# A four-part convolution kernel: attention weights carried to the lanes by DMA through DRAM, and the steps of the attention part ordered anew

## The chip, the cores and the metric

The kernel runs on one core of a Trainium2 chip. A core has five engines, each with its own stream of instructions taken in order: TensorE (PE, matrix products; its weight loads, PEld, overlap them), VectorE (DVE), ScalarE (ACT, functions from tables), GpSimd (POOL) and SyncE (SP, which here only issues transfers). Sixteen DMA engines move data between DRAM, which holds inputs, outputs and scratch tensors, and SBUF, the 128-lane working memory. Products are written to PSUM, eight banks of 512 floats a lane. Engines wait for each other on semaphores. The metric is the time of one execution in microseconds (us); smaller is better.

## What is computed

The input x is 8 images of 16 channels and 128 x 128 pixels, float32. Four layers follow, each of the form x = x + layer(group_norm(x)). The change lies in the first. For each pixel it takes the 3 x 3 window (wrapped at the border) as three tokens (the columns j of the window) of 48 numbers each (three rows, 16 channels), runs a small transformer block over the three tokens, and sums them:

```python
x = _fold_to_kernels(in_x)                     # [B*H*W, 3 tokens, 48]
h = _ln(x)
q, k, v = jnp.split(h @ w_attn.T, 3, axis=-1)  # then 4 heads of 12
att = jnp.einsum('nhtd,nhsd->nhts', q, k) * (1.0 / np.sqrt(HEAD_DIM))
att = jax.nn.softmax(att, axis=-1)
y = jnp.einsum('nhts,nhsd->nhtd', att, v)
x = x + y @ w_attn_proj.T
h = _ln(x)
x = x + jax.nn.gelu(h @ w_fc.T, approximate=False) @ w_fc_proj.T
x = _ln(x)
x = jnp.sum(x, axis=1).reshape(B, H, W, N_EMBD)
out = jnp.einsum('bhwc,oc->bohw', x, conv_w) + conv_b[None, :, None, None]
```

The second layer gates the pixels by two 1 x 1 convolutions, the third is a convolution of rational functions, the fourth one of splines. Their code does the same work in both kernels.

## The kernel before

Attention works in 32 steps of four image rows (`Step`, one chunk of 512 pixels per image). Lanes hold two images of 64 lanes each (48 used); four image pairs `k` make two halves `d`, each a tile of 128 lanes and 2 x 512 columns. A token `u` (0 to 2) of all four pairs is three half-tiles; so a step has six units, numbered `i = 3 d + u`.

The stages of a step are methods. `load` brings the input rows into `xin` (24 transfers of 32 KB). `center` (L441) multiplies by weights that also apply the group norm and subtract the mean; ACT copies the result and squares it. `first` adds the squares into the variances. `scaled` spreads the reciprocal deviation to all lanes and multiplies (DVE); `qkv` makes q, k and v in three products, copied out by ACT, with the wrapped border columns of k and v by POOL, and the differences `dv` of neighbouring columns of v. `multiply` (L483) forms q times the five shifted k, on POOL in the even middle. `scores` adds them over a head's lanes by PE into PSUM banks 1 and 0. `softmax` (L510) copies score rows together so that each of 96 rows has its three partners, subtracts the maximum, takes exponentials, adds (POOL), takes the reciprocal and multiplies (DVE). Only two of three weights are needed, since the three sum to one: y is the middle v plus weighted differences.

`attend` (L532) spreads the weights of one image pair `k` and one side `j` to the 128 lanes: three matmuls with a selection matrix `spread` into three banks; DVE multiplies by `dv` out of PSUM (L543), and POOL subtracts (L551) or adds (L553) to form y. There are eight such calls a step. `project` (L556) multiplies y by the projection weights, and DVE adds the centred input; `square` and `vary` feed the second variance. `normed`, `hidden` (two products of 128 outputs and one of 64, each with a gelu on ACT) and `back` are a unit of the second half; `unit` is a generator over them. The same squares and variances serve the last norm; `narrow` and `finish` apply the output weights and the last norm, `store` adds the input and writes the rows to the scratch tensor `x1d`.

All variances of a step (four kinds, of three steps at once) lie in one bank, and `Variances.finish` turns them into `rstd` by logarithm, exponential and two DVE operations. `place` says at which lane and row a variance lies: four groups of 32 lanes.

`two()` hands out pairs of banks in a ring of three pairs (two pairs while `attend` holds banks 1 to 3). A pair that is handed out again must first be emptied by ACT or DVE.

The main loop (L688) writes out the order of PE by hand: `in_turn` chains PE's instructions, and DVE's and POOL's heavy ones, in the order in which they are recorded. The other instructions are placed by a scheduling layer, which also sets each engine's final order. In one pass of the loop `new` is in attention, `old` in its last units and `then` in its q, k, v and scores, `ahead` in its centring. Eight slots `between` put the work of `old` (units 4 and 5) beside the eight `attend` calls, and projections, squares, variances and q, k, v of the next step behind them; after `rstd` come units 0 and 1 of `new` with the scores of `then`, its softmax beside unit 2, and unit 3.

ACT holds one table of functions at a time: `lut` (L143) orders the gelus and the exponentials and logarithms in phases, and a change of phase is a table load.

At the start, weights are loaded on ACT's queue (L297 to L319); the weights of the second part (`w1s`, 40 small blocks) and the biases are put into the list `loads`, which goes out on SP's queue in step 0 (L734).

Of the kernel before, what the change touches and what calls it, by code (L numbers as in the profile page):

```python
# [22 lines left out]
E = 48  # L23
# [13 lines left out]
def _constants():  # L37
# [19 lines left out]
    score = np.zeros((128, 56))  # L57
    score[token, 24 + 4 * g + h] = 1.0
    parts["score"] = score
    spread = np.zeros((128, 4, 128))  # L60
    bcast = np.zeros((128, 5, 128))
    last = np.zeros((128, 2, 2, 32))
    for t in range(4):
        bcast[32 * t + 16 + g, 4, token] = 1.0
        for n in range(4):
            bcast[32 * t + 4 * (n // 2) + 2 * (n % 2) + g, n, token] = 1.0
            spread[32 * t + 8 * n + 4 * g + h, n, token] = 1.0
        for u in range(2):
            for k in range(2):
                last[32 * t + 8 + 4 * u + 2 * k + g, u, k, 16 * g + c] = 1.0  # L70
    parts["spread"] = spread.reshape(128, 512)
    parts["bcast"] = bcast.reshape(128, 640)
# [33 lines left out]
def kernel(  # L106
# [29 lines left out]
    from_ = _WHERE["pair"][1]  # L136
    const = cpool.tile([128, _CONST.shape[1] - from_], F32, name="const")
    nc.scalar.dma_start(const, const_in[:, from_:])

    def k_(name):  # L140
        n, lo, hi = _WHERE[name]
        return const[:n, lo - from_ : hi - from_]
# [83 lines left out]
    w1s, b1s = [], []  # L226
    for n in range(5):
        t = cpool.tile([BC, BC], F32, name=f"w1_{n}")
        nc.gpsimd.memset(t, 0.0)
        for b in range(B):  # L230
            r = slice(b * C, (b + 1) * C)
            loads.append((t[r, r], w1[n].rearrange("i o -> o i") if n < 2 else w1[n]))
        w1s.append(t)
        b1s.append(rep(b1[n], B, f"b1_{n}"))
# [7 lines left out]
    with ExitStack() as l0:  # L242
# [19 lines left out]
        def k0(name):  # L262
# [4 lines left out]
        spread, bcast = (  # L267
            k0(name).rearrange("p (n m) -> p n m", m=128) for name in ("spread", "bcast")
        )
        last_sel = k0("last").rearrange("p (u k m) -> p u k m", u=2, k=2)  # L270
# [26 lines left out]
        for i in range(3):  # L297
            for g in range(2):
                r = slice(64 * g + i * 16, 64 * g + i * 16 + 16)
                nc.scalar.dma_start(  # L300
                    wqkv[r, :, :E], w0_qkv[i].rearrange("c (n o) -> c n o", n=3)
                )
                nc.scalar.dma_start(wfc[r], w0_fc[i])
                nc.scalar.dma_start(wcv[r, g * 16 : (g + 1) * 16], w0_conv[i])
# [11 lines left out]
        for g in range(2):  # L316
            nc.scalar.dma_start(wpc[64 * g : 64 * g + E, :E], w0_proj)
# [39 lines left out]
        def work(name):  # L357
            return tmp.tile([128, 2, 512], F32, tag="work", name=name, bufs=11)

        def large(name):  # L360
            return tmp.tile([128, 3, 512], F32, tag="large", name=name, bufs=5)
# [22 lines left out]
        def place(k, u):  # L384
            return 32 * (2 * (k % 2) + u % 2), 4 * (u // 2) + 2 * (k // 2)

        class Variances:
# [3 lines left out]
            def __init__(self, first, others):  # L391
                self.due = [first + n * others for n in (4, 2, 4, 2)]
                self.begun = [False] * 4
# [13 lines left out]
            def finish(self):  # L407
                w, pv = work("r0"), banks[:, 0]
                r0, sq = w[:, 0], w[:, 1]
                lut(r0, pv, AF.Ln, bias=eps_t, scale=-2.0)  # L410
# [3 lines left out]
                r = act.tile([128, 512], F32, name="rstd", bufs=2)  # L414
# [3 lines left out]
        class Step:  # L418


            def __init__(self, h0):
# [3 lines left out]
                self.dv = {}  # L425
# [16 lines left out]
            def center(self, d):  # L442
                p = two()
                blocks(p, lambda k: wcen[:, 2 * d + k], xin[:, 2 * d : 2 * d + 2])
                self.xc[d] = act.tile([128, 2, 512], F32, name="xc", bufs=5)
# [4 lines left out]
            def first(self, var):  # L450
                for d in range(2):
                    for k in range(2):
                        var.add(32 * (2 * d + k), 16, self.sq1[d][:, k])

            def scaled(self, d):
                p = two()
                for k in range(2):
                    t = 32 * (2 * d + k)
                    pe(p[:, k], bcast[t : t + 32, 4], self.r1[t : t + 32], start=True, stop=True)
# [3 lines left out]
            def qkv(self, d):  # L463
                q = self.q[d] = work("q")
                self.k[d] = act.tile([128, 8, W + 4], F32, name="kp", bufs=2)
                self.v[d] = act.tile([128, 8, W + 4], F32, name="vp", bufs=2)
                for n, t in enumerate((q, self.k[d], self.v[d])):
# [10 lines left out]
                    else:  # L478
                        copy(t, p)
                self.dv[d] = act.tile([128, 8, W + 4], F32, name="dv", bufs=2)  # L480
# [3 lines left out]
            def multiply(self, d, engine):  # L484

                for k in range(2):
                    parts = []
                    for at, n in ((0, 3), (3, 2)):
                        t = large("pd")
                        ins = (nc.vector if engine == "dve" else nc.gpsimd).tensor_mul(  # L490
                            t[:, :n].rearrange("p n (a b) -> p n a b", a=4),
# [7 lines left out]
            def scores(self, k, which):  # L499

                for i in which:
                    pe(
                        banks[32 * i : 32 * i + 32, 1] if i < 4 else banks[64:96, 0],
                        score[:, 24 - 8 * k : 56 - 8 * k],
# [5 lines left out]
            def softmax(self):  # L510

                a = self.att = act.tile([96, 3, 512], F32, name="att")
                for u in range(3):
                    copy(a[32 * u : 32 * u + 32, 1], banks[32 * u + 32 : 32 * u + 64, 1])
                copy(a[0:64, 2], banks[64:128, 1])
                copy(a[64:96, 2], banks[64:96, 0])
                w = work("mx")
                mx, sm = w[:96, 0], w[:96, 1]
                nc.vector.tensor_max(mx, banks[0:96, 1], a[:, 1])
                nc.vector.tensor_max(mx, mx, a[:, 2])  # L520
                nc.vector.tensor_sub(a[:, 0], banks[0:96, 1], mx)
                for j in (1, 2):
# [1026 lines left out]
```

## Time and profile before

| | |
|---|---|
| median of 3 runs | 10,415.76 us (10,415.72 to 10,424.08) |
| the profiled execution | 10,417.28 us |
| its span, first to last instruction | 10,415.5 us |
| PE busy | 8,808.0 us (85%) |
| DVE, ACT, POOL busy | 8,490.1, 8,595.5, 5,545.7 us |
| mean granted PE clock | 0.979 of full speed |
| first and last `rstd` (attention) | 59.6 and 3,184.9 us |
| first gate product of the second part | 3,213.4 us |
| moved by DMA | 215.74 MB, on average 21 GB/s |

The span is that of one execution; engines overlap in it, so busy times do not add up to it. The page cuts the span into 40 slices and gives each engine's busy share in tenths. Attention fills the first twelve slices, the rational convolution most of the rest. A row of a group of instructions gives the line, engine, operation, output and inputs with shapes, count, total busy us, mean ns of one, and the idle time of the engine before them with what ended it. Almost all matmuls of attention are recorded at one line (L375, the helper `pe`), so they are told apart by the names of their operands.

In the middle of attention, DVE, ACT, POOL and PE are busy 49.1, 52.2, 61.1 and 87.8 us a step (window 1000 to 1096 us). SP issues the 24 input loads in 16.1 us of queue time, and one load and one store of 256 KB.

### The profile page before, as it was taken

What the parts mean: (1) busy time and instruction counts of PE and PEld (TensorE: products, weight loads), DVE (VectorE), ACT (ScalarE), POOL (GpSimd) and SP (SyncE); (2) the same over time, 40 slices, a digit from 0 to 9 for tenths busy, and PEclk for the clock granted to TensorE, in tenths of its full rate; (3) what the DMA queues carried; (4) which work ended last, traced back from release to release, by engine and by line L of the source; (5) the groups of instructions that cost most, each with busy time, mean ns of one, the idle gap of its engine ahead of it and who ended that gap; (6) DMA issues with size and microseconds to landing.
All of it is one profiled execution on the core that took longest, in us unless ns stands there. A gap on an engine that the chain in (4) does not pass through costs nothing.

```text
span 10415.5 us, 192029 instructions
## 1 busy us (share of the span) xinstructions
PE 8808.0 (85%) x81400; PEld 2482.8 (24%) x81400; DVE 8490.1 (82%) x6774; ACT 8595.5 (83%) x7107; POOL 5545.7 (53%) x2608
## 2 busy tenths in 40 slices
PE   6999999999996888888888888888888888888799
PEld 1222222222222222222222222222222222222222
DVE  4545554554555999999999999999999999999977
ACT  3555555555555999999999999999999999999988
POOL 4666666666652555555555555555555555555421
PEclk8999999999998999999999999999999999999999
DMA  1000000000002000000000000000000000000022
GB/s 53 13 15 15 14 14 15 15 13 15 15 7 77 14 21 16 18 21 14 21 14 21 14 20 21 14 21 14 21 14 21 17 18 20 14 13 9 14 62 62
DMA packets 203668, 215.74 MB, mean 21 GB/s; under 512 B 50616, under 2 KB 159416, under 8 KB 200760
## 3 DMA queue, kind: packets, MB, share of 16 engines
q1 hardware_dynamic: 197544, 198.27, 7.0%
q8 instruction: 640, 10.49, 0.4%
q10 hardware_dynamic: 5264, 5.17, 0.2%
q14 instruction: 220, 1.80, 0.1%
HBM read 117.80 MB, written 60.04 MB: 17 GB/s over the span
## 4 chain that ended last, share of the span: by engine, by line
DVE 43%; PE 25%; issue 21%; ACT 8%; DMA 2%; SPq 1%; POOL 0%; DVEq 0%; ACTq 0%; POOLq 0%
PE banks L375 18%; DVE u L1078 15%; DVE pn L1078 10%; DVE u L1082 9%; DVE t L1068 2%; PE pn L1019 2%; PE pd L1019 2%; PE acc L1398 2%; DVE y L543 2%; DVE x L565 1%; ACT hid L157 1%; ACT sq L571 1%; ACT u L157 1%; DMA f<-yd 1%; DVE x L662 1%
## 5 line engine op out<-in xcount | busy, mean ns | idle before, releaser
L1091 POOL TENSOR_TENSOR v<-t,u 128x1280 f32<-128x1280 f32 x1152 | 3449.8, 2995 | 3080.8 <-DVE t L1068 3044.7
L1068 DVE SCALAR_TENSOR_TENSOR t<-t,u 128x2048 f32<-128x2048 f32 x1152 | 2632.7, 2285 | 32.3 <-ACT u L157 31.2
L1019 PE MATMUL pd<-f,wb 32*64 32x512 f32 x18432 | 2510.2, 608 | 92.8 <-ACT t L1057 40.5
L1057 ACT ACTIVATE t<-pd 128x1024 f32<-128x1024 f32 x2304 | 2364.9, 1026 | 133.2 <-PE pd L1019 75.0
L1019 PE MATMUL pn<-f,wa 32*64 32x512 f32 x18432 | 1299.4, 615 | 1112.1 <-DVE u L1082 1111.9
L157 ACT ACTIVATE u<-u 128x2048 f32<-128x2048 f32 x1152 | 2208.9, 1917 | 0.0
L157 ACT ACTIVATE u<-t 128x2048 f32<-128x2048 f32 x1152 | 2204.0, 1913 | 0.0
L1078 DVE TENSOR_TENSOR u<-pn,u 128x1280 f32<-128x1280 f32 x1152 | 1718.8, 1492 | 122.2 <-DVE pn L1078 2.8
L157 ACT ACTIVATE hid<-banks 128x1024 f32<-128x1024 f32 x576 | 569.9, 1023 | 1049.6 <-PE banks L375 1048.3
L1110 PE MATMUL acc<-u,const 128*32 128x512 f32 (+2 forms) x13824 | 1112.1, 454 | 0.0
L1078 DVE TENSOR_TENSOR pn<-pn,u 128x768 f32<-128x768 f32 x1152 | 1103.3, 958 | 0.0
L1082 DVE SCALAR_TENSOR_TENSOR u<-t,pn 128x768 f32<-128x768 f32 x1152 | 1087.6, 944 | 0.0
L1019 PEld LDWEIGHTS pd<-f,wb 32*64 32x64 f32 x18432 | 615.1, 130 | 1249.6 <-ACT t L1057 891.8
L1019 PEld LDWEIGHTS pn<-f,wa 32*64 32x64 f32 x18432 | 275.7, 130 | 2117.2 <-DVE u L1082 2109.7
L1110 PE MATMUL acc<-v,const 128*32 128x512 f32 (+1 forms) x9216 | 763.2, 449 | 1.5 <-POOL v L1091 1.5
L490 POOL TENSOR_TENSOR pd<-q,kp 128x1536 f32<-128x1536 f32 x248 | 674.6, 2732 | 11.2 <-PE banks L375 9.1
L571 ACT ACTIVATE sq<-x 128x1024 f32<-128x1024 f32 x384 | 395.3, 1053 | 272.6 <-DVE x L565 172.8
L375 PE MATMUL banks<-h,wfc 64*128 64x512 f32 (+1 forms) x3072 | 598.5, 617 | 14.6 <-DVE h L638 14.6
L638 DVE TENSOR_TENSOR h<-banks,x 128x1024 f32<-128x1024 f32 x192 | 232.6, 1211 | 428.2 <-PE banks L375 219.2
L543 DVE TENSOR_TENSOR y<-banks,dv 128x1536 f32<-128x1536 f32 x256 | 448.2, 1751 | 140.4 <-PE banks L375 134.1
L1110 PEld LDWEIGHTS acc<-u,const 128*32 128x32 f32 x13824 | 366.6, 109 | 812.6 <-issue 812.6
L553 POOL TENSOR_TENSOR y<-y 128x1536 f32<-128x1536 f32 x128 | 442.1, 3454 | 197.8 <-DVE y L543 197.5
(198 smaller groups left out, 8370.6 us busy)
## 6 DMA issues: line engine op xcount, KB each, us to landing
f<-yd SPq DMA_DIRECT2D x1016, 60.9 KB
yd<-y SPq DMA_DIRECT2D x280, 130.0 KB
xin<-in_x SPq DMA_DIRECT2D x744, 32.0 KB
four<-sil SPq DMA_DIRECT2D x256, 65.0 KB
xj<-in_x SPq DMA_DIRECT2D x8, 1024.0 KB
s<-in_x SPq DMA_DIRECT2D x32, 256.0 KB
x1d<-s SPq DMA_DIRECT2D x32, 256.0 KB
x<-x1d SPq DMA_DIRECT2D x8, 1024.0 KB
```

The source lines that it names most:

```text
L157: ins = nc.scalar.activation(out_, in_, func, **kw).ins
L375: in_turn("pe", mm(*args, skip_group_check=True, **kw).ins)
L490: ins = (nc.vector if engine == "dve" else nc.gpsimd).tensor_mul(t[:, :n].rearrange("p n (a b) -> p n a b", a=4), rows(self.q[d][:, k]).un ...
L543: ins = nc.vector.tensor_mul(out_, banks[:, at : at + 3].rearrange("p n (a b) -> p n a b", a=4), windows(dv, j // 2, 3),).ins
L571: nc.scalar.activation(self.sq[d][u], self.x2[d][:, u], AF.Square)
L1019: yield mm(p[64 * (u % 2) : 64 * (u % 2) + 64, u // 2], w[lo : lo + 32, q % 2, n].rearrange("p c f -> p (c f)"), fs[k * NP + q][lo : lo + ...
L1057: in_turn("act", nc.scalar.activation(self.t[:, ab], self.pd, AF.Abs).ins)
L1068: ins = nc.vector.scalar_tensor_tensor(self.t, self.t, 1.0, self.u, op0=ALU.add, op1=ALU.mult).ins
L1078: in_turn("dve", nc.vector.tensor_mul(u if cols.start else p, p, u).ins)
L1082: ins = nc.vector.scalar_tensor_tensor(u, t, 2.0, p, op0=ALU.subtract, op1=ALU.mult).ins
L1091: ins = nc.gpsimd.tensor_mul(self.v, t, u).ins
L1110: ins = mm(accs[k][32 * q : 32 * q + 32, lo % 512 : (hi - 1) % 512 + 1], gather[:, int(part == 1), g], flat(c.u)[:, ab, lo:hi] if src is N ...
```

## The change

- Attention weights: `attend`, its selection matrix `spread` and the tiles of `large` go. `softmax` ends with four transfers on SP's queue that write the two weight planes, each twice, to a scratch tensor in DRAM, `shared`. `fetch` reads for one unit 16 rows of 8 KB, each to eight lanes, into a tile `y` of 1 MB (two buffers), on SP's queue. `weigh` makes y of it by three DVE operations in SBUF: the product with `dv` of both sides, a subtraction and an addition of v. POOL has no part in it.
- Lanes: the heads of q, k, v lie at 16 lanes each, not 12. The weights for q, k, v and for the projection are therefore loaded in smaller pieces (18 transfers in place of 6, and 8 in place of 2, on ACT's queue).
- Variances: three lane groups of 32, rows of the fifth score at lanes 96 to 127 of the same bank; `rstd` is a tile of 96 lanes.
- Order: five steps are in flight. Softmax and scores are for the step after the next one (`ahead`), its last instructions at the end of the pass; the six weighings and projections of `then` stand one beside each of the six units of `new`. `two()` always has three pairs. There is one phase of exponentials and logarithms a pass.
- Storage: nine work tiles, not eleven; `store` uses the tile `z`; the write to `x1d` is a call of its own.
- The weights of the second part, and the constants that only later parts use, are loaded after attention, on ACT's queue.

The diff, cut to its core:

```diff
-    score = np.zeros((128, 56))
-    score[token, 24 + 4 * g + h] = 1.0
+    score = np.zeros((128, 62))
+    score[64 * g + 16 * h + r % HD, 30 + 2 * (4 * g + h)] = 1.0
...
         def place(k, u):
-            return 32 * (2 * (k % 2) + u % 2), 4 * (u // 2) + 2 * (k // 2)
+            return 32 * ((u + k) % 3)
...
-                self.due = [first + n * others for n in (4, 2, 4, 2)]
+                self.due = [first * n + 4 * others for n in (2, 1, 1)]
...
+                self.shared = dram.tile([6, 8, 2, 2, 2, 512], F32, name="shared", bufs=2)
+                for j in range(2):
+                    for i in range(2):
+                        nc.sync.dma_start(
+                            self.shared[:, :, i, j].rearrange("t h k m -> (t h) k m"), a[:, j]
+                        )
+
+            def fetch(self, d, u):
+                y = self.y[d, u] = tmp.tile([128, 2, 2, 512], F32, name="y", bufs=2)
+                nc.sync.dma_start(
+                    y.rearrange("p j k m -> p (j k m)"),
+                    self.shared[2 * u + d]
+                    .rearrange("h i j k m -> (h i) (j k m)")
+                    .unsqueeze(1)
+                    .to_broadcast([16, 8, 2048]),
                 )
+
+            def weigh(self, d, u):
+                y = self.y[d, u]
+                out_ = y.rearrange("p j k (a b) -> p j (k a) b", a=4)
+                in_turn("dve", nc.vector.tensor_mul(out_, out_, windows(self.dv[d], u, 2)).ins)
+                in_turn("dve", nc.vector.tensor_sub(y[:, 0], y[:, 1], y[:, 0]).ins)
+                at = out_[:, 0]
+                ins = nc.vector.tensor_add(at, at, self.v[d][:, :, u + 1 : u + 1 + W]).ins
+                in_turn("dve", ins)
...
+            do(new, "normed", 0)
+            do(old, "finish")
+            unit(0)
+            do(ahead, "scaled", 0)
+            back(0)
+            do(far, "load", 0)
+            do(ahead, "qkv", 0)
+            weigh(0)
+            do(ahead, "multiply", 0, engine)
...
+            unit(1)
+            back(1)
+            weigh(1)
+            project(0)
+            do(ahead, "scaled", 1)
+            unit(2)
+            back(2)
+            project(1)
+            weigh(2)
+            do(ahead, "qkv", 1)
...
+            do(old, "store")
+            back(3)
+            do(new, "square", 0)
+            project(2)
+            weigh(3)
...
+            do(ahead, "scores", 3, range(5))
+            soft = ahead.softmax() if ahead else iter(())
+            next(soft, None)
+            do(new, "square", 1)
+            project(5)
+            do(far, "center", 1)
+            do(ahead, "differ", 1)
+            do(new, "vary", 1, 1, var)
+            do(then, "square", 1)
+            end(soft)
+            do(far, "first", 1, var)
+            do(then, "vary", 1, 0, var)
+            if any((new, then, far)):
                 r = var.finish()
...
+            for j in range(2):
+                do(ahead, "fetch", *divmod(j, 3))
+            end(do(new, "narrow") or ())
...
+        w1s = []
+        for n in range(5):
+            t = wp.tile([BC, BC], F32, name=f"w1_{n}")
+            nc.gpsimd.memset(t, 0.0)
+            for b in range(B):
+                r = slice(b * C, (b + 1) * C)
+                nc.scalar.dma_start(t[r, r], w1[n].rearrange("i o -> o i") if n < 2 else w1[n])
+            w1s.append(t)
```

In the new loop `unit(i)` is `hidden(i)` and `normed(i + 1)`, `back(i)` is the sum of unit `i - 1` followed by the third product and gelu of unit `i`, `project(j)` is the projection of unit `j` followed by `fetch` of unit `j + 2`, and `weigh(j)` weighs unit `j`.

## The prediction

> **What bounds the kernel now.** First the slices of the page, which say where the attention part lies, then a thousand microseconds of its even middle by engine.
>
> ```profile
> span 10415.5 us, 192029 instructions
> PE   6999999999996888888888888888888888888799
> DVE  4545554554555999999999999999999999999977
> 1000.00:2000.00 1000.00, 913.23 (x5536) 252.19 (x5530) 506.81 (x414) 547.91 (x576) 639.14 (x360) 0.98 0.06 15
> ```
>
> Only the first twelve slices (260 us each) are attention. There the columns after the window are PE, PEld, DVE, ACT, POOL, clock, DMA share, GB/s: PE is busy 91%, DVE and ACT about half, the DMA engines 6%. PE sets the pace, so time is PE work plus PE's idle time. One step is 95.8 us by the timeline (the hidden layer's first matmuls begin at 1032.32, 1128.28, 1223.95); 0.913 of it is 87.5 us work, 8.3 us idle.
>
> Then the groups of 1000 to 1960 us (ten steps), shapes apart; last columns are total us, mean ns, idle before and its cause:
>
> ```profile
> L375 PE MATMUL banks<-att,const 32*128 32x512 f32 x480 | 104.2, 646 | 28.9 <-DVE y L543 15.8 <-DVE att L529 13.1
> L543 DVE TENSOR_TENSOR y<-banks,dv 128x1536 f32<-128x1536 f32 x80 | 140.1, 1751 | 40.4 <-PE banks L375 40.0
> L528 DVE RECIPROCAL mx<-mx 96x512 f32<-96x512 f32 x10 | 33.5, 3349 | 37.3 <-POOL mx L527 37.3
> L529 DVE TENSOR_TENSOR att<-att,mx 96x1024 f32<-96x1024 f32 x10 | 12.1, 1208 | 0.0
> L571 ACT ACTIVATE sq<-x 128x1024 f32<-128x1024 f32 x120 | 123.9, 1053 | 75.4 <-DVE x L565 43.6 <-DVE x L662 30.3
> L372 ACT ACTIVATE att<-banks 32x512 f32<-32x512 f32 x40 | 23.6, 589 | 0.7
> L553 POOL TENSOR_TENSOR y<-y 128x1536 f32<-128x1536 f32 x40 | 138.2, 3455 | 63.4 <-DVE y L543 63.4
> L1068 DVE SCALAR_TENSOR_TENSOR t<-t,u 128x2048 f32<-128x2048 f32 x1090 | 2491.0, 2285 | 31.4 <-ACT u L157 30.3
> ```
>
> The softmax chain (reciprocal 3.35 us on DVE) costs PE only 1.3 us a step: gelu units run beside it. (The last row is of the third part, and serves as a price.)
>
> **What is removed.** Per step, 24 spreading matmuls in eight groups; in the timeline of PE such a group goes from 1002.69 to the next at 1003.76, so 8 x 1.07 = 8.6 us of PE. With them go eight DVE products (14.0 us) and eight POOL passes (4 x 3.46 + 4 x 3.20 = 26.6 us), and two of four table loads (2.6 us of ACT); these three engines have slack, so I count nothing. PE gains one round of variance matmuls (0.9 us): rows now share three column groups, not four. PE work becomes 87.5 - 8.6 + 0.9 = 79.8 us.
>
> **What is added: prices.** A weigh is three DVE operations with all operands in SBUF: 2048 wide as the row L1068, 2.29 us, and two of 1024 as L529, 1.21 each; 4.7 us, six times 28.2, so DVE goes from 49 to 63 us. The spread is now four writes to DRAM (196 KB each) and six fetches of 1 MB, all on SP's queue. No row shows such a fetch; its bounds come from these (SP's waits between 3100 and 3400 us, two windows of the reload of x, and DVE beside POOL at the start):
>
> ```profile
> SPq L794 <- DMA x1d<-s: 3.2, 1, 3.2
> 3188.00:3191.00 3.00, 0.00 (x0) 0.00 (x0) 0.04 (x1) 0.00 (x0) 2.84 (x5) 0.65 0.95 352
> 3194.00:3197.00 3.00, 1.14 (x4) 1.00 (x4) 0.96 (x6) 0.00 (x0) 0.00 (x0) 0.50 0.98 258
> 70.59 1.95 POOL L482 TENSOR_TENSOR dv<-vp 128x1055 f32<-128x1055 f32 x1
> 71.51 2.64 DVE L490 TENSOR_TENSOR pd<-q,kp 128x1536 f32<-128x1536 f32 x1
> 76.09 1.76 DVE L490 TENSOR_TENSOR pd<-q,kp 128x1536 f32<-128x1536 f32 x1 [0.81 <-POOL kp L476]
> ```
>
> A 256 KB write was waited for 3.2 us; 0.75 us of that is bytes at 352 GB/s, so about 2.4 is fixed. A fetch is then 0.33 (issue) + 2.4 + 1.05 MB at 352 GB/s (3.0) = 5.7 us, at 258 GB/s 6.8. The shortest wait for a landing in the trace is 1.6 us (SP's last, for an output): with 416 GB/s, the best five-microsecond window, that gives 4.4; the slowest window, 211 GB/s, gives 7.7. I take 5.8, between the two reload rows. The last two lines: a DVE operation on two SBUF operands takes 1.76 us alone and 2.64 us when POOL is in one; 71.51 + 2.64 - 1.76 = 72.4 is about when POOL ends. So each weigh may also wait for POOL.
>
> [...]
>
> **Where PE will stand still.** The program's order (each engine's instructions, with what each waits for) is fixed, so stalls can be walked.
>
> 1. Start of a step, after softmax's last product on DVE. Four writes issue in 1.3, the last lands 3.2 later, the fetch 5.8: 10.3. DVE's next in order is weigh(0), and behind it h2 of unit 1 and the product of scaled(0): 2.29 + 1.21 + 1.21 + 1.21 + 1.22 = 7.1, so qkv(0) can begin at 17.5. PE meanwhile has normed, finish, hidden(0), normed with scaled, third(0): 1.06 + 1.92 + 1.95 + 2.12 + 1.02, from 0.7 on: 8.8. Stall 8.7.
> 2. Fetch 2 starts when project(0) ends; weigh(2) heads DVE's queue. DVE: 5.9, product 2.29, h2 1.21: 9.4; PE has normed, scaled, hidden, back, third = 7.9 before project(1), whose bank pair h2 must free: 1.5. Then DVE sub, add and back(1)'s sum end at 13.0, PE wants qkv(1) at 10.4: 2.6. Store (2.1) and one sum end at 16.4, the third qkv group could begin at 15.1: 1.3. On SP the x1d write, which waits for the store, stands before fetch 3: issue 14.2, landing 20.0, weigh and h2 25.9, against PE at 24.3: 1.6. Sum 7.0; POOL collisions another 1.3 (the second half of a dv pass, 0.9, and once 0.4).
> 3. Unit 5: copy and square of center(0), then three squares, 5.2 us of ACT, before the last variance matmuls; PE has 4.4 with the tail of matmuls at 6.5: 2.1.
> 4. Tail: after the last scores ACT makes five score copies (2.95), three squares, center's two, three squares: 11.3, and 1.2 of matmuls follow; PE has project, center and variances, 6.7. Stall 5.8.
> 5. Behind the last square: exponential 1.48, two POOL sums 2.52, reciprocal 3.35, the variance product 0.70 (behind it in DVE's order), softmax product 1.21, rstd 0.69, six hand-overs of 0.05: 10.3. PE has 1.2 and narrow 2.7. Stall 6.4. In the kernel before, units covered this chain; here no unit stands behind it.
>
> Step: 79.8 + 8.7 + 8.3 + 2.1 + 5.8 + 6.4 = 111.1 us, 15.3 more than 95.8. With 30 full steps (3125 us from the first rstd at 59.6 to the last at 3184.9 hold 32.6 periods, the ends thinner) that is +459.
>
> **The ends.** At the start ACT's queue issues 18 more weight loads at 0.576 us, 10.4 us, ahead of the square root at 42.2, which had some 6 us of room: +4. Behind attention, 40 loads of the second part's weights (0.42 us each on SP before, in the shade of step 0) and one constant now stand on ACT's queue before the eight bs loads that DVE's chain waits for (11.6 us there before, throttled by landings of x): at best the bs loads run unthrottled, +9, at worst all are throttled alike, +34; I take +22, the middle. Third and fourth part keep their instructions: 0.
>
> Sum against the profiled span: 10,415.5 + 459 + 4 + 22 = 10,900 us. The median of the runs, 10,415.76, is within 0.3 us of that span, so nothing is added.
>
> **Rivals.**
> - PE still paces everything and its idle stays 8.3: 88.1 a step, -231, with the ends 10,210. For it: PE is 91% busy and loses work. Against: stalls 1, 4 and 5 are chains in written order. It decides from the point where both fetches of a step's start land before DVE wants them and the tail's 11.3 us of squares is covered; 0.05.
> - The DMAs are as good as hidden: stall 1 is DVE alone (7.1 from 5.1, against 8.8: 3.4), stall 2 only 1: 98.5 a step, 10,520. For it: the engines are 6% busy. Against: fetch 0 waits for the softmax itself; 0.08.
> - The fetch is much slower (16 rows read eight times each, after fresh writes): 3 us more in stall 1, 3 in each of two fetches of stall 2, and 5 from the fetches of units 4 and 5, where DVE's slack ends: 125 a step, 11,320. For it: the 211 GB/s window; against: reload of a scratch tensor at 352; 0.17.
> - My forecast, with its own range 10,720 (fetch 4.4, write 2.0: stall 1 6.0, stall 2 5.5, +9.8 a step, ends +13) to 11,090 (fetch 7.7: 117.1 a step, ends +38): 0.70.
>
> Range 10,640 to 11,210: it leaves most of the first rival and the upper half of the third out. About 0.2% is what a measurement of this kernel tells from no change. Faster 0.06 (the first rival and a little), same 0.02, slower 0.92.
>
> **What would show it.** Attention's last rstd near 3,650 instead of 3,185; a period near 111; PE waiting for hn at every step's start (about 9 us), for rstd (6) and for squares (6 and 2); DVE waiting for fetches at every weigh; POOL near 34 us a step. I am wrong if PE stays above 85% busy there, or if hn's wait is under 4 us.

## The result, and the profile after

The changed kernel takes 11,076 us (median; 11,075 to 11,083), the kernel before in the same runs 10,418 us: ratio 1.0632, 95% interval 1.0614 to 1.0651. It is slower, as forecast, and inside the range of 10,640 to 11,210, but 176 us above the 10,900 of the forecast.

First the head of the page of the changed kernel with three of its rows of slices (277 us each):

```profile
span 11081.7 us, 189286 instructions
...
PE   5778777787787678888888888888888888888899
...
DVE  5555555555555479999999999999999999999977
...
PEclk8888888888888889999999999999999999999999
```

Then its even middle by engine (columns after the window: PE, PEld, DVE, ACT, POOL, clock, DMA share, GB/s):

```profile
1000.00:2000.00 1000.00, 780.94 (x4088) 199.93 (x4090) 566.06 (x434) 418.26 (x446) 302.07 (x226) 0.87 0.31 74
```

The part with attention now fills fourteen slices, and PE is busy 78% of it instead of 91%. PE's clock is the new thing: 0.87 where the kernel before had 0.98. From the first to the last rstd there are 3,756.9 us (before: 3,124.6), so this stretch has 632.3 of the 666.2 us by which the span grew; 6.7 lie ahead of it (first rstd at 66.3 instead of 59.6) and 27.2 behind it (7,258.5 from the last rstd to the end instead of 7,231.3). One step, from rstd's first matmuls at 1004.13 to the next ones at 1119.85, takes 115.7 us; it was 95.8.

The groups of ten steps (1004 to 2164 us) that answer to those shown of before (last columns: total us, mean ns, idle before and its cause), with the qkv group of PE:

```profile
L553 DVE TENSOR_TENSOR y<-y,dv 128x2048 f32<-128x2048 f32 x60 | 138.4, 2306 | 263.7 <-DMA y<-shared 263.7
...
L574 ACT ACTIVATE sq<-x 128x1024 f32<-128x1024 f32 x120 | 119.0, 1053 | 10.4 <-DVE x L667 10.1
...
L369 PE MATMUL banks<-hn,wqkv 64*64 64x512 f32 x480 | 100.0, 996 | 117.7 <-DVE hn L456 85.2 <-DVE x L667 32.5
...
L556 DVE TENSOR_TENSOR y<-y,vp 128x1024 f32<-128x1024 f32 x60 | 89.6, 1494 | 1.7
...
L554 DVE TENSOR_TENSOR y<-y 128x1024 f32<-128x1024 f32 x60 | 82.3, 1372 | 1.4
...
L527 DVE RECIPROCAL mx<-mx 96x512 f32<-96x512 f32 x10 | 33.5, 3349 | 96.4 <-POOL mx L526 96.4
```

DVE waits for a fetch ahead of the weighs, 26.4 us a step. Reciprocal and squares cost what they did (3.35 and 1.05 us), but ACT hardly waits ahead of the squares now (10.4 us in ten steps instead of 75.4): it is PE that waits for them. The two operations of 1024 take 1.37 and 1.49 us in the mean instead of 1.21: beside POOL's dv (20 and 10 of the 60) they take 1.67 and 2.85 us, the others 1.22. The 24 matmul records of a qkv (each matmul of the program leaves two) take 5.32 and 5.01 us in the step shown next; in an experiment below they take 2.81, in the kernel before 3.16 (1020.20 us, granted clock 1.00).

The start of that step on PE (start, duration, what; in brackets the wait before and who ended it):

```profile
1004.13 3.99 PE L369 MATMUL banks<-rstd,const 32*128 32x512 f32 x28 [5.29 <-DVE rstd L409]
1008.05 3.12 PE L369 MATMUL banks<-h,wfc 64*128 64x512 f32 x8
...
1022.32 5.32 PE L369 MATMUL banks<-hn,wqkv 64*64 64x512 f32 x24 [8.22 <-DVE hn L456]
```

The stalls stand where they were foreseen: 5.29 us for rstd, 8.22 for hn. But the first two groups and qkv run slowly. The clock in the same stretch, cut at multiples of 3.41 us (columns as above):

```profile
1000.13:1003.54 3.41, 0.00 (x0) 0.00 (x0) 3.41 (x4) 0.00 (x0) 0.00 (x0) 1.00 0.00 0
1003.54:1006.95 3.41, 2.82 (x16) 0.76 (x28) 1.23 (x2) 0.00 (x0) 0.00 (x0) 0.50 0.59 179
1006.95:1010.37 3.42, 3.42 (x30) 1.13 (x8) 2.35 (x3) 1.47 (x2) 0.38 (x2) 0.50 0.34 104
1010.37:1013.78 3.41, 3.41 (x20) 1.02 (x16) 0.00 (x0) 1.86 (x2) 2.36 (x2) 1.00 1.07 250
1013.78:1017.19 3.41, 0.32 (x4) 0.00 (x0) 1.88 (x1) 1.02 (x1) 0.00 (x0) 1.00 0.99 223
...
1020.60:1024.02 3.42, 1.70 (x8) 0.55 (x12) 3.42 (x3) 0.00 (x0) 0.00 (x0) 0.50 0.02 5
1024.02:1027.43 3.41, 3.41 (x20) 0.74 (x12) 2.89 (x3) 2.05 (x2) 0.27 (x2) 0.50 0.00 0
...
1041.08:1044.50 3.42, 1.92 (x18) 0.48 (x16) 2.16 (x1) 1.02 (x1) 0.00 (x0) 1.00 0.00 0
1044.50:1047.91 3.41, 1.09 (x8) 0.21 (x8) 3.38 (x4) 0.00 (x0) 1.95 (x1) 1.00 0.00 0
1047.91:1054.74 6.83, 4.49 (x24) 1.24 (x24) 5.36 (x6) 1.76 (x2) 0.00 (x0) 0.50 0.42 114
```

The clock is 1.00 or 0.50 and changes at these cuts alone. In this step it falls behind windows in which PE worked 0, 0.32 and 1.09 us, stays up behind one of 1.92, and rises behind one that was full (3.41; behind 2.82 and 1.70 it stayed at 0.50). So in this step a wait costs PE twice: by itself, and by up to 6.2 us at half speed behind it (1004.13 to 1010.37).

These figures are no thresholds. Two pairs of windows from later steps of the same trace:

```profile
1235.65:1239.07 3.42, 3.42 (x28) 0.35 (x26) 1.23 (x1) 0.39 (x1) 0.00 (x0) 0.50 0.75 230
1239.07:1242.48 3.41, 3.41 (x20) 1.13 (x8) 1.82 (x2) 1.91 (x2) 1.33 (x3) 0.50 0.51 130
...
1952.45:1955.87 3.42, 2.87 (x16) 1.04 (x20) 3.38 (x3) 0.82 (x1) 0.00 (x0) 0.50 0.00 0
1955.87:1959.28 3.41, 3.41 (x22) 1.07 (x16) 1.76 (x2) 3.07 (x5) 1.77 (x3) 1.00 0.00 0
```

A full window was not followed by the full clock, and one with 2.87 us of work was. In the kernel before, a window with 1.91 us of work at 1.00 (1058.95 to 1062.37) was followed by one at 0.50. What the clock answers to is not shown here.

### The profile page after: what moved, and what is told of

The parts are those of the page before. It is cut to its first block, busy times and chain, and to the rows that moved or that the text cites. A ratio compares the mean times of both kernels' runs of the same rounds, so it can differ in the third digit from the quotient of the medians.

```text
span 11081.7 us, 189286 instructions
## 1 busy us (share of the span) xinstructions
PE 8867.5 (80%) x79864; PEld 2457.3 (22%) x79864; DVE 9024.0 (81%) x7094; ACT 8508.6 (77%) x7045; POOL 4758.0 (43%) x2352
## 4 chain that ended last, share of the span: by engine, by line
DVE 43%; issue 22%; PE 16%; DMA 9%; ACT 5%; SPq 2%; POOL 1%; DVEq 0%; ACTq 0%; POOLq 0%
DVE u L1081 15%; PE banks L369 11%; DVE pn L1081 9%; DVE u L1085 9%; DMA y<-shared 7%; DVE t L1071 2%; DVE y L553 2%; PE pn L1022 2%; DVE y L554 1%; ACT sq L574 1%; PE pd L1022 1%; PE acc L1401 1%; DVE h L643 1%; DMA shared<-att 1%; ACT att L366 1%
## 5 line engine op out<-in xcount | busy, mean ns | idle before, releaser
L1060 ACT ACTIVATE t<-pd 128x1024 f32<-128x1024 f32 x2304 | 2358.8, 1024 | 130.0 <-PE pd L1022 66.0
L553 DVE TENSOR_TENSOR y<-y,dv 128x2048 f32<-128x2048 f32 x192 | 447.4, 2330 | 817.1 <-DMA y<-shared 817.1
L369 PE MATMUL banks<-h,wfc 64*128 64x512 f32 (+1 forms) x3072 | 632.5, 639 | 15.8 <-DVE h L643 12.1
L369 PE MATMUL banks<-hn,wqkv 64*64 64x512 f32 x1536 | 311.6, 973 | 361.3 <-DVE hn L456 261.7
L369 PE MATMUL banks<-sq,const 128*32 128x512 f32 x1792 | 482.7, 610 | 67.7 <-ACT sq L574 47.8
L369 PE MATMUL banks<-rstd,const 32*128 32x512 f32 (+1 forms) x1792 | 375.9, 847 | 182.9 <-DVE rstd L409 182.6
```

Source lines behind the costliest of these rows:

```text
L369: in_turn("pe", mm(*args, skip_group_check=True, **kw).ins)
L553: in_turn("dve", nc.vector.tensor_mul(out_, out_, windows(self.dv[d], u, 2)).ins)
L1060: in_turn("act", nc.scalar.activation(self.t[:, ab], self.pd, AF.Abs).ins)
```

## The experiments

Nine kernels were run, each beside the kernel before. "First to last rstd" (35 of them) is the stretch that the step sets, "behind" the time from the last rstd to the end, both from the profiled run; the clock is the one granted in 1000 to 2000 us.

| kernel | median us | ratio to before, 95% interval | first to last rstd | behind | clock |
|---|---|---|---|---|---|
| before | 10,416 to 10,418 | | 3,124.6 | 7,231.3 | 0.98 |
| changed | 11,076 | 1.0632, 1.0614 to 1.0651 | 3,756.9 | 7,258.5 | 0.87 |
| hn_first | 10,819 | 1.0387, 1.0371 to 1.0402 | 3,486.4 | 7,258.3 | 0.91 |
| no_fetch | 10,598 | 1.0175, 1.0160 to 1.0191 | 3,273.5 | 7,258.4 | 0.94 |
| fill | 11,019 | 1.0578, 1.0562 to 1.0593 | 3,679.4 | 7,261.9 | 0.95 |
| hn_rstd_first | 10,966 | 1.0525, 1.0507 to 1.0543 | 3,660.3 | 7,261.1 | 0.88 |
| pd_on_dve | 10,580 | 1.0164, 1.0149 to 1.0180 | 3,254.9 | 7,256.8 | 0.96 |
| tail_on_dve | 10,437 | 1.0021, 1.0012 to 1.0030 | 3,111.6 | 7,247.0 | 0.95 |
| recip_on_act | 10,414 | 0.9999, 0.9990 to 1.0008 | 3,091.1 | 7,249.4 | 0.95 |
| sums_first | 10,363 | 0.9949, 0.9937 to 0.9962 | 3,049.1 | 7,247.6 | 0.95 |
| sums_first_fill | 10,352 | 0.9938, 0.9925 to 0.9952 | 3,053.8 | 7,247.7 | 0.96 |

### hn_first: is stall 1 a term of its own?

```diff
-                nc.vector.tensor_mul(self.hn, p, self.xc[d])
+                in_turn("dve", nc.vector.tensor_mul(self.hn, p, self.xc[d]).ins)
...
-                nc.vector.tensor_mul(self.h2[i], p, self.x2[d][:, u])
+                in_turn("dve", nc.vector.tensor_mul(self.h2[i], p, self.x2[d][:, u]).ins)
```

> The edit puts the products that make h2 and hn into the same written order on DVE as the weighs, so that in each step h2 of unit 1 and hn of pair 0 come ahead of weigh(0) and no longer wait behind fetch 0. Nothing else is moved by hand. In the changed kernel the period is 115.7 us; PE waits 8.2 us for hn, and its qkv(0) then runs 5.32 us instead of 3.16. The forecast's reading (each wait is a term of its own): the 8.2 us go, qkv(0) runs at full clock (2.2 us), and 2 to 3 us come back because weigh(0) and weigh(1) now stand ahead of h2 of unit 2. Period 108 us, total 11,076 - 32 x 7.5 = 10,836 us, range 10,760 to 10,920. Rival (one chain, softmax to writes to fetch 0 to weigh(0) to project(0), sets the step, and whatever PE does earlier is waited for again at project(0)): period 113 to 116 us, total 10,980 to 11,080.

Measured: 10,819 us, 257 less; two rstds lie 105.8 to 109.6 us apart between 1000 and 2200 us (changed: 115.4 to 118.2). PE's wait for hn is 0.59 us, the qkv behind it takes 2.81 us. The total is that of the forecast's reading, and the rival's 10,980 to 11,080 is out. But the edit takes every h2 (the product of `normed`) out of the weighs' way, not only that of unit 1: in 1000 to 2000 us PE's waits for hn fall from 77.5 to 5.3 us, those for h2 from 49.8 to 0.5, and those for the sums behind the weighs rise from 31.6 to 96.2. So the 257 us are not stall 1 alone. What is left is seen in a stretch of the timeline, DVE's and POOL's lines:

```profile
2041.60 8.42 POOL L487 TENSOR_TENSOR pd<-q,kp 128x1536 f32<-128x1536 f32 x2
...
2045.08 2.73 DVE L553 TENSOR_TENSOR y<-y,dv 128x2048 f32<-128x2048 f32 x1
2047.84 3.26 DVE L554 TENSOR_TENSOR y<-y 128x1024 f32<-128x1024 f32 x1
...
2051.03 1.21 DVE L667 TENSOR_TENSOR x<-banks,x 128x1024 f32<-128x1024 f32 x1
2051.25 6.39 POOL L487 TENSOR_TENSOR pd<-q,kp 128x1536 f32<-128x1536 f32 x2
...
2052.16 3.26 DVE L556 TENSOR_TENSOR y<-y,vp 128x1024 f32<-128x1024 f32 x1
```

The fetch of the second unit is in time here, but the two engines hold each other up: POOL's pair of products took 5.40 us in the changed kernel and takes 8.42, the weigh's operations of 1.22 us take 3.26, while the sum L667, which reads PSUM, takes its 1.21. Over 1000 to 2000 us the means are 2,427, 1,874 and 2,486 ns; against 2,283 (in pd_on_dve below), 1,220 and 1,220 undisturbed that is 2.06 us a weigh, 12.4 a step. By what means they do it is not shown.

### no_fetch: what is the way through DRAM worth?

The weigh's first product takes a constant of SBUF, and the fetch is gone, so the sums are not weighted by the softmax:

```diff
-                nc.sync.dma_start(
-                    y.rearrange("p j k m -> p (j k m)"),
-                    self.shared[2 * u + d]
...
-                in_turn("dve", nc.vector.tensor_mul(out_, out_, windows(self.dv[d], u, 2)).ins)
+                even = bcast[:, 0].unsqueeze(1).unsqueeze(1).to_broadcast([128, 2, 8, W])
+                in_turn("dve", nc.vector.tensor_mul(out_, even, windows(self.dv[d], u, 2)).ins)
```

> The six fetches of a step are left out; the weigh's product takes a constant from SBUF in place of the fetched weights, in the same size. So the sums are not weighted by the softmax; every other operation and the four writes stay. The forecast's reading (waiting for transfers is most of the loss): stall 1 (8.2 us) falls to about 1, the waits for h2 and for the sum behind weigh(2) and weigh(3) (2.8 + 3.3 + 2.7 us) to about 3, and qkv and the groups after run at full clock (about 5 us): period 98 to 102 us, total 10,520 to 10,640 us, still slower than before (10,418) by the tail's squares and the softmax chain. Rival (transfers are cheap, the loss is DVE's added work and the order of the tail): period above 110 us, total above 10,900.

Measured: 10,598 us, inside the first theory's range. Without any fetch 478 of the 658 us are gone. Of the span's 181 us that remain, 149 lie between the first and the last rstd and 32 at the ends. PE's waits of 1000 to 2000 us (total, times, longest):

```profile
PE banks L369 <- DVE rstd L409: 51.2, 9, 5.7
PE banks L369 <- DVE hn L456: 27.4, 20, 2.2
PE banks L369 <- DVE x L661: 19.1, 10, 1.9
PE banks L369 <- DVE h L637: 17.4, 10, 1.7
PE banks L369 <- ACT sq L568: 15.0, 10, 1.5
```

The softmax chain ahead of rstd is the largest, untouched by the fetches. So the new pipeline, with transfers that cost nothing, is still slower than the kernel before, though it has fewer matmuls. But the 478 us are not the whole price of the fetches, for a loss takes their place. DVE no longer waits, and weighs and POOL's work both take longer, as in hn_first (POOL is busy 447.9 us of 1000 to 2000 us, 302.1 in the changed kernel):

```profile
L547 DVE TENSOR_TENSOR y<-const,dv 128x2048 f32<-128x2048 f32 x60 | 198.8, 3313 | 0.0
L548 DVE TENSOR_TENSOR y<-y 128x1024 f32<-128x1024 f32 x60 | 124.9, 2081 | 1.4
L550 DVE TENSOR_TENSOR y<-y,vp 128x1024 f32<-128x1024 f32 x60 | 110.8, 1847 | 1.4
```

Against 2,283, 1,220 and 1,220 ns undisturbed this is 2.5 us a weigh, 15 a step, where the changed kernel loses 2.7. pd_on_dve below, with all its fetches but without these products on POOL, is 18 us faster than no_fetch.

### fill: does the half clock cost time?

```diff
+        def fill(n):
+            for _ in range(n):
+                rhs = bcast.rearrange("p n m -> p (n m)")[:64, :512]
+                pe(banks[:, 1], wfc[:64, 0:128], rhs, start=True, stop=True)
...
+            fill(8 if then else 0)
             do(ahead, "qkv", 0)
...
+            fill(2 if then else 0)
             project(1)
...
+            fill(3 if then else 0)
             do(ahead, "qkv", 1)
...
+            fill(2 if then else 0)
             project(2)
```

> Fifteen matmuls of no use (64 rows, 128x512 out, into a score bank that is free then) are added to each step: 8 before qkv(0), 2 before project(1), 3 before qkv(1), 2 before project(2), the places where PE stands waiting for DVE. The order on DVE stays. By the single-row-group price of about 0.95 us (two that share the array take 0.99) that is 14 us more work for PE, all of it inside waits of 8.2, 2.8, 3.3 and 2.7 us. Theory that PE's clock falls to half after a wait and that this costs time: the matmuls behind the waits run at full clock again (qkv(0) 3.16 us instead of 5.32, qkv(1) 3.16 instead of 5.01), the granted clock goes from 0.87 to above 0.93, and the step becomes 2 to 4 us shorter although PE does more: total 10,950 to 11,010. Theory that the clock only stretches matmuls whose end nobody waits for: total 11,070 to 11,130.

```profile
2025.18 7.13 PE L369 MATMUL banks<-const,wfc 64*128 64x512 f32 x16
2033.13 2.81 PE L369 MATMUL banks<-hn,wqkv 64*64 64x512 f32 x24 [0.81 <-DVE hn L461]
```

PE's timeline: the eight useless matmuls fill the wait, and the same qkv takes 2.81 us instead of 5.32. The clock of the stretch rises from 0.87 to 0.95, and the kernel is 58 us faster with 14 us more work for PE in every step (the useless matmuls take 124.4 us in 1000 to 2000 us, 0.93 each), a little less than foreseen (66 to 126). The rival's range begins at 11,070; it is out. The eight matmuls leave the 16 records of the first line; the wait for rstd has no filling, and the group behind it still takes 3.99 us; the scores behind project(2) take 3.30 us here, no less than the 2.89 in the changed kernel. But the price of the half clock is less than what the matmuls lose: the two qkv alone lose 2.51 and 2.20 us in the changed kernel, and nearly all of that is gone here (their mean falls from 1,007 to 650 ns in 1000 to 2000 us), yet the step became only 2.4 us shorter (77.5 us over some 32 steps between first and last rstd in the profiled runs; by the medians, 58 us, it is 1.8). What PE gained beyond that it did not turn into time; that it waits for it again at the next fetch is the likely reading, not a measured one.

### hn_rstd_first: is stall 5 a term of its own?

```diff
-                nc.vector.scalar_tensor_tensor(pv, pv, -0.5 * EPS, sq, op0=ALU.add, op1=ALU.mult)
+                in_turn("dve", nc.vector.scalar_tensor_tensor(pv, pv, -0.5 * EPS, sq, op0=ALU.add, op1=ALU.mult).ins)
...
-                nc.vector.reciprocal(sm, sm)
+                in_turn("dve", nc.vector.reciprocal(sm, sm).ins)
...
-            end(soft)
...
             if any((new, then, far)):
                 r = var.finish()
...
+            end(soft)
```

> hn_first, and the variance products on DVE ahead of the softmax's reciprocal instead of behind it (the reciprocal and the softmax product now come after rstd; the scheduler puts h2 of unit 0 between them). To be read against hn_first. The forecast's reading (stall 5 is a term of its own): PE's wait for rstd falls from 5.3 us to about 1, so the period falls by 3.5 to 4.3 us, total 110 to 135 us under hn_first. Rival (the chain through the softmax's writes and fetch sets the step): the softmax product ends 1.4 to 2.6 us later than in hn_first, so writes, fetch 0 and weigh(0) do too, and what PE gains at the start it loses at the wait behind weigh(0): within 40 us of hn_first, or slower.

Measured: 10,966 us, 147 more than hn_first: the rival holds, and by more than its numbers. DVE's timeline at the start of a step:

```profile
1999.87 0.69 DVE L409 SCALAR_TENSOR_TENSOR rstd<-banks,r 96x512 f32<-96x512 f32 x1
2000.48 3.34 DVE L527 RECIPROCAL mx<-mx 96x512 f32<-96x512 f32 x1
...
2004.82 1.21 DVE L528 TENSOR_TENSOR att<-att,mx 96x1024 f32<-96x1024 f32 x1
...
2020.52 3.51 DVE L553 TENSOR_TENSOR y<-y,dv 128x2048 f32<-128x2048 f32 x1 [6.20 <-DMA y<-shared]
2024.07 3.25 DVE L554 TENSOR_TENSOR y<-y 128x1024 f32<-128x1024 f32 x1
```

PE waits only 0.99 us for rstd, but the softmax product ends 5.5 us behind rstd, where it ended just ahead of it, and so does everything that hangs on it: fetch 0 lands at 2020.5, its weigh falls into POOL's products, and PE stands 4.91 and 6.39 us behind it. Stall 5 is not a term of its own: the way from the softmax to project(0) runs beside it, and it is longer.

### pd_on_dve: are the collisions what is left?

```diff
-            def multiply(self, d, engine):
+            def multiply(self, d, engine, ks=range(2)):
...
-                for k in range(2):
+                for k in ks:
...
-            engine = "pool" if then else "dve"
+            engine = "dve"
...
-            do(ahead, "multiply", 0, engine)
...
             unit(2)
+            do(ahead, "multiply", 0, engine, (0,))
...
             weigh(2)
+            do(ahead, "multiply", 0, engine, (1,))
...
-            do(ahead, "multiply", 1, engine)
...
             do(ahead, "scores", 0, range(5))
+            do(ahead, "multiply", 1, engine, (0,))
...
             do(ahead, "scores", 1, range(5))
+            do(ahead, "multiply", 1, engine, (1,))
```

(on top of hn_first)

> hn_first, and the products pd of query and key (POOL: 5.4 us for the two of one plane, four times a step) go to DVE, cut into four calls of 2.95 us (1.75 and 1.2) spread between the units, so that POOL runs no long product beside the weighs. To be read against hn_first (10,819 us, period 106.2), where the weigh's operations of one step took 12.9 us longer than alone (3.26, 3.50, 4.03 us for those of 1.22) and PE waited 10.1 us a step for sums that stand behind them on DVE. Theory that collisions of DVE and POOL are what is left of the loss behind the fetches: the weighs run at 2.29 and 1.22 us, PE's waits for sums fall by 5 to 8 us a step, period 98 to 101, total 10,560 to 10,660 us. Rival (DVE has no room: it takes on 11.8 us of products for the 12.9 it is rid of, and the sums wait behind these instead): total 10,780 to 10,900 us.

Measured: 10,580 us, 239 less than hn_first, two rstds 98.6 to 100.6 us apart between 1000 and 2200 us. PE's waits for sums in 1000 to 2000 us fall from 96.2 to 43.0. DVE's groups of 1000 to 2000 us:

```profile
L553 DVE TENSOR_TENSOR y<-y,dv 128x2048 f32<-128x2048 f32 x61 | 139.3, 2283 | 15.4 <-DMA y<-shared 15.3
L556 DVE TENSOR_TENSOR y<-y,vp 128x1024 f32<-128x1024 f32 x61 | 90.8, 1489 | 1.1
L554 DVE TENSOR_TENSOR y<-y 128x1024 f32<-128x1024 f32 x61 | 83.5, 1369 | 1.4
```

The weighs are near their price again (what stays is probably POOL's dv: the means of 1.37 and 1.49 us are those of the changed kernel), and DVE does the products of one plane in 1.75 + 1.21 us where POOL needed 5.40 undisturbed. DVE had the room. The edit also moves the products to other places in the written order; what that alone is worth was not measured.

### tail_on_dve, recip_on_act: stalls 3, 4 and 5

```diff
-            do(then, "square", 1)
+            do(then, "square", 1, "dve")
...
-                    nc.gpsimd.tensor_sub(t, t, mx)
+                    nc.vector.tensor_sub(t, t, mx)
...
-                nc.gpsimd.tensor_add(sm, left, middle)
-                nc.gpsimd.tensor_add(sm, sm, right)
+                nc.vector.tensor_add(sm, left, middle)
+                nc.vector.tensor_add(sm, sm, right)
...
-            do(far, "first", 0, var)
-            do(then, "vary", 0, 0, var)
             back(5)
             project(4)
             weigh(5)
             do(ahead, "scores", 2, range(5))
+            do(far, "first", 0, var)
+            do(then, "vary", 0, 0, var)
...
-                nc.scalar.dma_start(t[r, r], w1[n].rearrange("i o -> o i") if n < 2 else w1[n])
+                nc.sync.dma_start(t[r, r], w1[n].rearrange("i o -> o i") if n < 2 else w1[n])
```

> pd_on_dve, and three edits of the end of a step: the last three squares of the tail (pair 1 of the step whose sums are dealt out) on DVE instead of ACT, the softmax's two differences and two sums on DVE instead of POOL, the variances of pair 0 one unit later; and the 40 loads of the second part's weights on SP's queue instead of ACT's. Forecast's reading (stalls 3, 4 and 5 are real and lie in ACT's squares and in the chain to rstd): ACT's tail shortens by 2.95 us and the softmax chain by about 1.2, PE's wait for rstd falls from 5.3 to about 2 us and no half-clock stretch follows it: 5 to 6 us a step less, 160 to 190 us; behind attention, from the last rstd to the end, 10 to 20 us less than the 7,258 us of the changed kernel. Total 10,380 to 10,470 us: level with the kernel before (10,416). Rival (the way of softmax, writes, fetch 0 and weigh(0) sets the step, so that an earlier rstd is waited for again at project(0)): within 50 us of pd_on_dve.

Measured: 10,437 us; 143 us less from first to last rstd (4.4 a step, where 5 to 6 were expected) and 9.8 less behind it. PE's wait for rstd is 25.4 us in ten waits instead of 52.8. So a shorter chain to rstd is worth time here. hn_rstd_first had bought an earlier rstd with a later softmax; these edits shorten both. Which of them gave how much was not tried one by one.

```diff
-                nc.vector.reciprocal(sm, sm)
+                lut(sm, sm, AF.Ln)
+                lut(sm, sm, AF.Exp, scale=-1.0)
```

> tail_on_dve, and the softmax's reciprocal (3.35 us on DVE) is made on ACT as the exponential of the negative logarithm (two activations of 96x512, 0.65 us each). The softmax's product and with it writes and fetch 0, and the variance product behind it, come 2 us earlier. If this chain still sets the step: 1 to 2 us a step, 30 to 65 us under tail_on_dve. If it is covered by now: within 20 us.

Measured: 23 us less, between the two expectations; PE's wait for rstd stays (26.0 us in eleven waits), so the gain probably came from the earlier fetch 0; no run shows that by itself.

### sums_first, sums_first_fill: the rest of the order

```diff
-                nc.vector.tensor_add(self.x2[d][:, u], p, self.xc[d])
+                in_turn("dve", nc.vector.tensor_add(self.x2[d][:, u], p, self.xc[d]).ins)
...
-                nc.vector.tensor_add(x2, p, x2)
+                in_turn("dve", nc.vector.tensor_add(x2, p, x2).ins)
...
-            weigh(1)
             project(0)
             do(ahead, "scaled", 1)
+            weigh(1)
```

> recip_on_act, and DVE takes the sums that PE waits for (of back and of project) in the written order too, with weigh(1) written behind the sum of project(0) instead of ahead of it. In recip_on_act PE waits in 1000 to 2000 us 33.5 + 15.5 us for such sums, 4.7 us a step, most of it (2.8 and 1.4 us) where the sum of back(0) stands behind the first operations of weigh(1). If order on DVE, not the fetches, is what is left of the loss: 2 to 3 us a step less, total 10,310 to 10,360 us, clearly under the kernel before (10,416). Rival (weigh(1) then comes late for project(1), and the wait only moves): within 20 us of recip_on_act (10,414).

Measured: 10,363 us, 0.5% under the kernel before (0.9937 to 0.9962), 51 under recip_on_act: 3 us above the range of the gain and well below the rival's. From first to last rstd it is 42 us, 1.3 a step where 2 to 3 were expected. PE's waits of 1000 to 2000 us:

```profile
PE banks L369 <- DVE x L672: 31.3, 11, 2.8
PE banks L369 <- DVE rstd L409: 25.9, 11, 2.4
PE banks L369 <- ACT vp L366: 18.0, 10, 2.2
```

The waits for sums fell from 49.0 us (two lines of sums) to 31.3, and part of it moved to the copy of vp, whose oldest buffer a weigh still reads (ACT waits 29.4 us for L557, the weigh's addition of v).

> sums_first, and two matmuls of no use (0.95 us each) ahead of the first normed of each step, where PE waits some 2.4 us for rstd. Clock theory: in recip_on_act hidden(0) behind that wait takes 3.79 us instead of 1.99 and the next two groups of rstd 2.35 instead of 2.1; with the wait filled they run at full clock in most steps: 1 to 2 us a step, 30 to 65 us under sums_first. Rival (what PE gains there it waits for again, since hn or weigh(0) ends later than PE comes): within 15 us of sums_first, or slower by what the two matmuls delay.

Measured: 10,352 us, and 4.7 us more from first to last rstd; the intervals overlap widely. The first group of rstd takes 2.17 us in every step from 1000 to 2000 us, where in sums_first it took 2.17, about 2.8 and 3.99 by turns; with hidden(0) behind it, that is 1.3 us a step less in the mean of ten steps. The wait for rstd falls to 4.9 us, and the wait for vp rises to 24.3. The rival holds: no time clear of the noise came of it.

## Why the prediction was right, and where it was off

The direction, the mechanism and the places were right; the 176 us are mis-sized terms. By its steps:

- **PE's work, 79.8 us: the step that failed.** It was priced at the durations of the kernel before, whose PE is busy 91% of 1000 to 2000 us at a granted clock of 0.98. Measured in the step 1004.13 to 1119.85: 91.45 us busy. Two runs of squares hold waits of their own inside (4.74 us for sixteen that take 2.77 in hn_first, and 8.16 for 27 at 0.16 each), 5.8 us; 9.4 are the half clock (rstd's first group 3.99 against 2.17 in sums_first_fill, hidden 3.12 against 1.99, qkv 5.32 and 5.01 against 2.81, project 1.76 against 1.04, scores 2.89 against 1.92). That leaves 76.3 at full clock: the matmuls themselves were priced 3.5 too high, and the clock was left out.
- **Stall 1, 8.7:** 8.22. Two errors cancel: the first weigh began 11.8 us behind the softmax's product instead of 10.3, and PE came 1.8 us later to the wait, since its first 6.2 us there ran at half clock. That they cancel is luck.
- **The fetch, 5.8 (4.4 to 7.7):** 7.0 us from issue (fetch 2 from 1035.3 to 1042.3), at 210 GB/s in 1036 to 1041 us, with the DMA engines 93% busy. The slow end of the bounds (211 GB/s) was the nearer row, not the reload of x.
- **Stall 2 with collisions, 8.3:** 2.83 + 3.34 + 2.72 = 8.9. The wait of 1.3 for the third qkv group did not come; the other three were longer than foreseen, by 1.3, 0.7 and 1.1 without their collisions. Fetch 3 was issued at 1051.33, right behind the x1d write at 1050.88, as walked. Collisions cost DVE (1,372 + 1,494 - 2 x 1,210 ns) x 6 = 2.7 us, not 1.3.
- **Stalls 3, 4 and 5, 2.1 and 5.8 and 6.4:** 2.0, 1.50 + 3.84 = 5.3, and 5.3. All idle time of the step: 24.3 + 5.8 = 30.1 us, forecast 31.3.
- **The sum, 111.1:** 115.7, that is +9.4 for the clock, -3.5 for the work, -1.2 for the stalls. This adds up as a record of one step. It does not say what PE would gain without the half clock: fill gave the two qkv nearly all of their 4.7 us back, and the step became 1.8 to 2.4 us shorter. That the stalls may be added up at all held only because they were taken as they stood together: hn_rstd_first took one away and lost time.
- **Thirty steps:** the stretch between first and last rstd grew by 632.3 us, 31.8 times the 19.9 of the step shown, not 30 times; the thin steps at the ends lose too. 35 us.
- **The ends, +4 and +22:** +6.7 and +27.2. ACT's queue after attention:

```profile
3825.67 33.37 ACTq L804 DMA_DIRECT2D w<-in_w  x40
3859.40 13.25 ACTq L848 DMA_DIRECT2D bs<-in_w_base  x8
3872.68 1.28 ACT L160 ACT_TABLE_LOAD   x1 [48.87 <-DMA dense<-in_a]
```

The 40 loads took 0.83 us each, not 0.42, and ACT's first function of the second part stands behind them, as do the bs loads. With the loads on SP's queue (tail_on_dve against pd_on_dve) 9.8 us went. Loading them in the shade of attention, as before, was not tried.

In sum: 4.6 us in thirty steps are 138, the count of steps adds 35, the ends 8. That is 181 of the 182 us between the profiled span, 11,081.7 us, and the forecast.

The signals: period 115.7 (near 111), last rstd at 3,823 (near 3,650), PE waiting for hn 77.5 us in nine waits, 8.6 each (about 9), for rstd 47.7 in nine, 5.3 each (6), DVE for most of the fetches, POOL 35 us a step (34), PE 78% busy (below 85). Of the rivals, PE's pace and hidden transfers are out by these waits. The slow fetch, 11,320, was nearest in time after the forecast, but its reason did not hold: the fetch is 1.2 us slower than taken, not 3 and more, and fetches 4 and 5 are no stall.

## What to carry to other kernels

An engine's queue in written order turns one late transfer into a wait for everything behind it: putting hn and h2 ahead of the weighs that wait for fetches was worth 257 us, without a change to the transfer. The stalls of one profile could be added up here as they stood, but the gain from removing one cannot be read off it: follow the other chain that ends at the same place first. And a change that makes the busiest engine wait should be priced at that engine's speed after a wait, not at its speed in a kernel where it seldom waits: here the same qkv took 5.32 us behind a wait of 8.22 and 2.81 behind one of 0.59 (hn_first).

## What was not expected of the hardware

TensorE's clock changed between 1.00 and 0.50 only at cuts 3.41 us apart. It fell behind windows in which PE still worked, 1.09 us of 3.41 in the step shown and 1.91 in the kernel before, and took 9.4 us of matmul time in that step; useless matmuls in the waits gave nearly all of the 4.7 us in the two qkv back, and 1.8 to 2.4 us of time. A fetch that reads each of 16 rows of 8 KB eight times moved 210 GB/s with the DMA engines 93% busy (1036 to 1041 us), where the reload of x moved 352 GB/s at 95% (3188 to 3191 us) and 258 at 98% (3194 to 3197 us). Without fetches to wait for, the weighs took 15 us a step more than undisturbed, against 2.7 in the changed kernel; with POOL's products moved to DVE (pd_on_dve) it was 2.5. An exponential of a negative logarithm on ACT in place of DVE's reciprocal of 96x512 (3.35 us) made tail_on_dve 23 us faster.
